# Eight layers on one core: the last sequence's state-space preparation under raised priority, and a softplus sum in another order

## The chip, the cores and the metric

The kernel runs on one core of a Trainium2 chip. Its engines are TensorE (PE, with its weight loads, PEld), VectorE (DVE), ScalarE (ACT), GpSimd (POOL) and SyncE (SP, which issues most DMAs). Each engine takes its instructions in the order in which the program lists them and waits on semaphores for the others. The metric is the device time of one execution in microseconds; the lower the better.

## The reference

A residual network of eight parts runs over x of 8 sequences x 256 positions x 128 channels, each followed by a layernorm of x + part(x): a gated linear recurrence, two layers of local attention, a selective state space, a mixture of 32 experts (top 1), attention in chunks, a mixture of 8 experts (top 2) with a shared expert, attention of typed heads and a ternary linear layer. The change touches the state space:

```python
xz = x @ W_in
x_inner, z = jnp.split(xz, 2, axis=-1)
xc = silu(causal depthwise convolution of x_inner, 4 taps, + conv_b)
x_ssm = xc @ W_xproj
delta_raw, Bm, Cm = x_ssm[..., :1], x_ssm[..., 1:17], x_ssm[..., 17:]
delta = jax.nn.softplus(delta_raw * w_dt + b_dt)
A = -jnp.exp(A_log)
dA = jnp.exp(delta[..., None] * A)
dBx = delta[..., None] * Bm[:, :, None, :] * xc[..., None]
# h = dA_t * h + dBx_t ;  y_t = sum_n h * C_t   over the 256 positions, 16 states
y = y + xc * D_param
y = y * jax.nn.silu(z)
return y @ W_out
```

## The kernel before

Channels lie on the 128 partitions and positions along the free dimension. One program runs six stages in a row; the change is in the second, `local_mamba`, in which the eight sequences pass through local attention and then the state space. Both are written as generators that yield their estimated cost; `interleave` runs four sequences of the first kind, staggered by 24, with up to two of the second behind them, and so sets the order in which instructions are written. A scheduler then gives every engine its own list: among the instructions that its model of the machine holds to be ready, it takes the one of the highest priority, which by default is the order of writing. `tc.high_priority()` raises the priority of what is issued inside it.

`mamba_sequence` (from L717) handles one sequence b. For both halves of 256 inner channels:

- L726 to L735: two matmuls into `xin`, then the convolution: ACT writes `xc` (L731), three DVE operations add the other taps (L733), first for one half, then for the other.
- L737 to L742: two matmuls into `z`, SiLU of `z` (`sz`) and of `xc` on ACT, then the loading of the exponential's table.
- L744 to L750: the 33 rows of x_ssm (`xps`, copied to `xs`), written to DRAM by SP.
- L761 to L778: `raw`, one matmul that spreads row 0 over all partitions, and the softplus. It is |v| and relu(v) for both halves (L767, L768: `e`, `r`), e = exp(-|v|) (L769), d = ln(1 + e) (L770), and a correction of the rounding in 1 + e: t = (e + 1) - 1 on DVE (L771), e = e - t, d = d + e, d = d + r, and u = d * xc. These last four (L774 to L778) run on POOL, but for the last sequence (b = 7) on DVE.
- L782 to L797, eight steps of two states each: SP fetches the rows of B and C from DRAM to all partitions (`bc`, 2 x 256 KB, three buffers, L758), ACT makes four `da` (L789, three buffers), DVE makes `hs` (L791), scans it (L793) and multiplies it by C (L794), PE adds it to `y`.
- L798 to L814: xc * D and SiLU of z (L800, L801), `wout`, the sum `s` (L806), a layernorm into `x_mamba`, and the router's logits (`lg`, L820).

Beside the last sequence runs `beside`: the folding of attention weights (`fold`, copied to `la_kq`, `la_vp`, `sa_kq`, `sa_vp` by ACT; `less`, `la_res`, `sa_res`), and, once sequence 6 is done, `route1` for its 14 tiles: comparisons on DVE (L961 to L967), a cumulative sum on PE (`cum`), transposes of the tiles (`rows`, L982, copied to `x_chunked` by ACT), the places (`put`, L993), and 14 indirect DMAs by POOL (L1088). After the last sequence `route1` runs once more for its two tiles; then SP and ACT load the experts' rows (`got`, L1108), and the stage `moe1` begins. SP also loads the expert weights (`w_moe`, L1135) in the order of writing.

Of the kernel before, what the change touches and what calls it, by code (L numbers as in the profile page):

```python
# [12 lines left out]
F32 = mybir.dt.float32  # L13
BF = mybir.dt.bfloat16
I32 = mybir.dt.int32
AF = mybir.ActivationFunctionType
ALU = mybir.AluOpType
# [4 lines left out]
P = 128  # L22
B = 8
S = 256
# [272 lines left out]
class _Kernel:  # L297
# [419 lines left out]
    def mamba_sequence(self, b, x, y, na, das, work, scan):  # L717


        nc = self.nc  # L720
        win = self.w1[:, 0:512]
        wx = self.w1[:, 512:578].rearrange("p (c f) -> p c f", c=2)
        wout = self.w1[:, 578:834].rearrange("p (c f) -> p c f", c=2)
        flat = lambda a: a.rearrange("p c s -> p (c s)")
        tile = lambda name, bufs=1: work.tile([P, 2, S], F32, tag="ma_" + name, name=name, bufs=bufs)
        ps = self.psum("M", "xin").rearrange("p (c s) -> p c s", c=2)  # L726
        for c in range(2):
            self.mm(ps[:, c, :], win[:, c * P : (c + 1) * P], x)
        xc = tile("xc", 2)
        for c in range(2):  # L730
            nc.scalar.activation(xc[:, c, :], ps[:, c, :], AF.Identity, scale=self.v("convw", 4 * c + 3), bias=self.v("convb", c))  # L731
            for k in range(1, 4):
                nc.vector.scalar_tensor_tensor(  # L733
                    xc[:, c, k:S], ps[:, c, 0 : S - k], self.v("convw", 4 * c + 3 - k), xc[:, c, k:S], ALU.mult, ALU.add
                )  # L735
        yield 2.0
        ps = self.psum("M", "z")  # L737
        for c in range(2):
            self.mm(ps[:, c * S : (c + 1) * S], win[:, 256 + c * P : 256 + (c + 1) * P], x)
        sz = tile("sz", 2)  # L740
        nc.scalar.activation(flat(sz), ps, AF.Silu)
        self.exp_ln(nc.scalar.activation(xc, xc, AF.Silu))  # L742
        yield 2.0
        ps = self.psum("M", "xps")  # L744
        for c in range(2):
            self.mm(ps[0:33, 0:S], wx[:, c, :], xc[:, c, :], c == 0, c == 1)
        xs = work.tile([33, S], F32, tag="xs", name="xs", bufs=2)
        nc.scalar.copy(xs, ps[0:33, 0:S])
        xd = self.dram.tile([33, S], F32, name=f"xs{b}")
        nc.sync.dma_start(xd, xs)  # L750

        def rows(m):

            bc = scan.tile([P, 2, 2, S], F32, tag="bc", name="bc", bufs=3)
            for k in range(2):
                r = 1 + 16 * k + 2 * m
                src = xd[r : r + 2, :].rearrange("n s -> (n s)").unsqueeze(0).to_broadcast([P, 2 * S])
                nc.sync.dma_start(bc[:, k].rearrange("p n s -> p (n s)"), src)  # L758
            return bc

        raw = self.psum("M", "raw")[:, 0:S]  # L761
        self.mm(raw, self.ident[0:33, 0:1].to_broadcast([33, P]), xs)
        yield 1.0

        e, r, d, t = tile("e"), tile("r"), tile("d", 2), tile("t")
        for c in range(2):
            nc.scalar.activation(e[:, c, :], raw, AF.Abs, scale=self.v("wdt", c), bias=self.v("bdt", c))  # L767
            nc.scalar.activation(r[:, c, :], raw, AF.Relu, scale=self.v("wdt", c), bias=self.v("bdt", c))  # L768
        nc.scalar.activation(e, e, AF.Exp, scale=-1.0)  # L769
        nc.scalar.activation(d, e, AF.Ln, bias=1.0)  # L770
        nc.vector.tensor_scalar(t, e, 1.0, -1.0, ALU.add, ALU.add)  # L771

        eng = nc.vector if b == B - 1 else nc.gpsimd
        eng.tensor_sub(e, e, t)  # L774
        eng.tensor_add(d, d, e)
        eng.tensor_add(d, d, r)
        u = tile("u", 2)
        eng.tensor_mul(u, d, xc)  # L778
        yield 3.0
        yp = self.psum("Y", "y")  # L780
        shp = [P, 2, 2, S]
        for m in range(8):  # L782
            bc = rows(m)
            bn, cn = (bc[:, k].unsqueeze(2).to_broadcast(shp) for k in range(2))
            da = das[m % len(das)]
            for n in range(2):
                for c in range(2):
                    i = 16 * c + 2 * m + n
                    nc.scalar.activation(da[:, n, c, 1:S], d[:, c, 1:S], AF.Exp, scale=na[:, i : i + 1])  # L789
            hs = scan.tile(shp, F32, tag="hs", name="hs", bufs=3)  # L790
            nc.vector.tensor_tensor(hs, u.unsqueeze(1).to_broadcast(shp), bn, ALU.mult)  # L791
            line = lambda a: a.rearrange("p n c s -> p (n c s)")
            nc.vector.tensor_tensor_scan(line(hs), line(da), line(hs), 0.0, ALU.mult, ALU.add)  # L793
            nc.vector.tensor_tensor(hs, hs, cn, ALU.mult)  # L794
            for n in range(2):
                self.mm(yp, self.ident, flat(hs[:, n]), m == 0 and n == 0, m == 7 and n == 1)
            yield 2.3  # L797
        yg = tile("t")  # L798
        for c in range(2):
            nc.vector.scalar_tensor_tensor(yg[:, c, :], xc[:, c, :], self.v("dpar", c), yp[:, c * S : (c + 1) * S], ALU.mult, ALU.add)  # L800
        eng.tensor_mul(yg, yg, sz)  # L801
        ps = self.psum("M", "wout")[:, 0:S]
        for c in range(2):
            self.mm(ps, wout[:, c, :], yg[:, c, :], c == 0, c == 1)
        s = work.tile([P, S], F32, tag="h2", name="s")
        nc.vector.tensor_add(s, ps, x)  # L806
        yield 2.0
        self.layernorm(work, s, y[:, bass.ts(b, S)])
        yield 2.0
        self.logits(b, y, self.w1[:, 834:866], self.lg1[0][:, 2 * b : 2 * b + 2] if b < 7 else self.lg1[1])  # L810
        self.done = b
        yield 1.0
# [1004 lines left out]
```

## Time and profile before

| | |
|---|---|
| Median of three runs | 1902.89 us (1902.8 to 1905.53) |
| Profiled execution | 1898.62 us, its span 1896.8 us |
| Mean granted clock of TensorE | 0.91 |
| Busy share of the span | PE 84%, PEld 50%, DVE 58%, ACT 54%, POOL 30% |
| Last scan step of sequence 6 multiplied by C (L794) | 839.2 us |
| First and last scan step of sequence 7 (L793) | from 861.95 us, to 898.3 us |
| First expert transposes | 921.33 us |

Times inside the profile are microseconds from the start of its span. A line of the order of time gives start, duration, engine, line, operation, output <- inputs, shapes, a count, and in brackets the idle time of the engine before it with what ended it. Matmuls of 32-bit data run in two passes, so a program's two matmuls appear as x4.

### The profile page before, as it was taken

The page shows a single profiled execution, that of the slowest core. Times are in us where ns is not written, and L with a number is a line of the kernel's source. Part 1 is how long each engine was busy: PE and PEld are TensorE (multiplying, and loading weights), DVE is VectorE, ACT ScalarE, POOL GpSimd, SP SyncE. Part 2 cuts the span into 40 slices and gives each one's busy share as a digit, 9 for nine tenths or more (in the row PEclk, how much of TensorE's full clock was granted, in tenths as well). Part 3 has the DMA queues.
Part 4 walks back from the last instruction along what each step waited for, and adds up shares of the span by engine and source line. Part 5 has one row for each costly group of instructions (what it writes and reads, how often), then busy time and mean ns, then how long its engine had stood idle before and what let it go on. Part 6 is the DMA issues. An engine that isn't in the chain of part 4 may idle for free. (4 is left out here: it accounts for less than half of the span.)

```text
span 1896.8 us, 28424 instructions
## 1 busy us (share of the span) xinstructions
PE 1585.0 (84%) x10810; PEld 957.3 (50%) x10810; DVE 1093.2 (58%) x2011; ACT 1020.7 (54%) x2702; POOL 560.4 (30%) x493
## 2 busy tenths in 40 slices
PE   3678887878788778786679999999988987899997
PEld 2344554535454444343656566665554733455554
DVE  5734458687779686679234554456443222467664
ACT  4557777667767877554234455444433312365654
POOL 1324443344342423203120211111111042255452
PEclk7789998989899988888789999999998997899998
DMA  4000002111112122366300000000101310000000
GB/s 172 1 1 1 1 35 56 35 56 35 45 46 56 35 56 68 95 215 167 102 24 2 10 6 6 6 5 5 36 2 29 104 39 13 1 4 4 7 4 9
DMA packets 58328, 75.50 MB, mean 40 GB/s; under 512 B 5868, under 2 KB 35236, under 8 KB 57168
## 3 DMA queue, kind: packets, MB, share of 16 engines
q1 hardware_dynamic: 52864, 67.57, 12.2%
q0 software_dynamic: 3216, 5.07, 0.9%
q8 instruction: 85, 1.39, 0.3%
q10 hardware_dynamic: 2112, 1.05, 0.2%
q14 instruction: 51, 0.42, 0.1%
HBM read 65.46 MB, written 9.71 MB: 40 GB/s over the span
## 5 line engine op out<-in xcount | busy, mean ns | idle before, releaser
L394 PE MATMUL y<-hs,ident 128*128 128x512 f32 x256 | 152.7, 727 | 38.0 <-DVE hs L794 37.8
L793 DVE TENSOR_TENSOR_SCAN hs<-da,hs 128x1024 f32<-128x1024 f32 x64 | 153.5, 2404 | 1.8 <-ACT da L789 1.6
L475 PE MATMUL pt<-ident,e 128*128 128x128 f32 x768 | 125.6, 291 | 23.7 <-POOL e L652 12.4
L652 POOL TENSOR_TENSOR e<-e,rc 128x1024 f32<-128x1024 f32 x32 | 67.9, 2121 | 232.6 <-DVE rc L651 232.6
L1686 ACT ACTIVATE e<-sc,nm 128x128 f32<-128x128 f32 (+1 forms) x256 | 104.1, 424 | 59.8 <-DVE nm L1681 57.5
L789 ACT ACTIVATE da<-d,na 128x255 f32<-128x255 f32 x256 | 111.8, 503 | 37.6 <-DVE hs L793 18.8
L1689 POOL TENSOR_TENSOR e<-e,rc 128x1024 f32<-128x1024 f32 x48 | 91.9, 1915 | 135.7 <-DVE rc L1688 102.4
L647 ACT ACTIVATE e<-sc,nm,rn 128x128 f32<-128x128 f32 x256 | 113.4, 462 | 24.9 <-DVE nm L642 22.4
L475 PEld LDWEIGHTS pt<-ident,e 128*128 128x128 f32 x768 | 90.2, 147 | 64.1 <-issue 22.4
L1298 POOL TENSOR_TENSOR e<-e,rc 128x512 f32<-128x512 f32 x32 | 33.5, 1048 | 295.7 <-DVE rc L1297 178.9
L599 POOL TENSOR_TENSOR t<-t,t 128x512 f32<-128x512 f32 x64 | 90.9, 1421 | 95.4 <-DVE t L586 79.0
L477 ACT COPY ptsb<-pt 128x512 f32<-128x512 f32 x94 | 55.1, 587 | 96.3 <-PE pt L475 87.5
L791 DVE TENSOR_TENSOR hs<-u,bc 128x1024 f32<-128x1024 f32 x64 | 86.2, 1357 | 34.0 <-POOL u L778 29.4
L394 PEld LDWEIGHTS y<-hs,ident 128*128 128x128 f32 x256 | 53.8, 226 | 97.6 <-DVE hs L794 51.7
L1273 ACT COPY kp<-kps 128x512 f32<-128x512 f32 x128 | 74.8, 584 | 41.7 <-PE kps L394 39.8
L1122 POOL DMA_INDIRECT got<-ybuf,get x48 | 45.5, 949 | 162.2 <-DMA ybuf<-ys 116.7
L477 DVE COPY ptsb<-pt 128x512 f32<-128x512 f32 x98 | 65.6, 685 | 33.5 <-PE pt L475 33.3
L394 PE MATMUL qk<-w_local,h 128*128 128x512 f32 x128 | 71.5, 648 | 14.1 <-DVE t L586 9.7
L794 DVE TENSOR_TENSOR hs<-hs,bc 128x1024 f32<-128x1024 f32 x64 | 80.0, 1256 | 0.2
L1246 DVE BATCH_NORM_STATS2 st<-out 128x6 f32<-128x128 f32 x80 | 20.0, 288 | 93.8 <-PE out L394 86.8
L1681 DVE TENSOR_REDUCE nm<-sc 128x4 f32<-128x1024 f32 (+1 forms) x48 | 58.6, 1220 | 24.6 <-PE sc L394 24.3
L1309 ACT COPY vs<-vps 128x512 f32<-128x512 f32 x64 | 37.4, 584 | 65.6 <-PE vps L394 44.1
(394 smaller groups left out, 3899.9 us busy)
## 6 DMA issues: line engine op xcount, KB each, us to landing
bc<-xs SPq DMA_DIRECT2D x128, 256.0 KB
w_attn<-in_w_dram SPq DMA_DIRECT2D x4, 1024.0 KB
w_local<-in_w_dram SPq DMA_DIRECT2D x2, 1557.0 KB
places<-zeros SPq DMA_DIRECT2D x2, 1280.0 KB
w_moe<-in_e1gate_dram SPq DMA_DIRECT2D x8, 256.0 KB
w_moe<-in_e1up_dram SPq DMA_DIRECT2D x8, 256.0 KB
w_moe<-in_e1down_dram SPq DMA_DIRECT2D x8, 256.0 KB
w_moe<-in_e2rg_dram SPq DMA_DIRECT2D x8, 256.0 KB
```

What stands on the lines that cost most here:

```text
L394: return self.nc.tensor.matmul(out, lhsT, rhs, start=start, stop=stop)
L475: self.last = self.nc.tensor.transpose(pt[:, j * P : (j + 1) * P], src[:, j * P : (j + 1) * P], self.ident)
L477: self.nc.any.tensor_copy(sb.rearrange("p a b -> p (a b)"), pt)
L599: nc.gpsimd.tensor_add(t1, t1, t2)
L647: nc.scalar.activation(e[:, j, g, :], scs[:, j, g, :], AF.Exp, bias=nm[:, j, g : g + 1], scale=rq[:, j, g : g + 1], accum_out=sm[:, j, g : ...
L789: nc.scalar.activation(da[:, n, c, 1:S], d[:, c, 1:S], AF.Exp, scale=na[:, i : i + 1])
L791: nc.vector.tensor_tensor(hs, u.unsqueeze(1).to_broadcast(shp), bn, ALU.mult)
L793: nc.vector.tensor_tensor_scan(line(hs), line(da), line(hs), 0.0, ALU.mult, ALU.add)
L794: nc.vector.tensor_tensor(hs, hs, cn, ALU.mult)
L1273: nc.scalar.copy(k[:, 2 * i : 2 * i + 2, :].rearrange("p a b -> p (a b)"), ps)
L1686: nc.scalar.activation(e[:, i, :], sc[:, i, :], AF.Exp, bias=nm[:, i : i + 1], accum_out=sm[:, i : i + 1])
L1689: nc.gpsimd.tensor_tensor(e, e, rc.unsqueeze(2).to_broadcast([P, n, keys]), ALU.mult)
```

## The change

For the last sequence (b = 7) the code up to `u` is put in `tc.high_priority()`; for the others the block is `ExitStack`, which does nothing. For all sequences the correction e - t is added to r, and that sum to d, where before it was added to d, and then r.

```diff
+        ahead = self.tc.high_priority if b == B - 1 else ExitStack
+        with ahead():
+            ps = self.psum("M", "xin").rearrange("p (c s) -> p c s", c=2)
...
         yield 2.0
-        ps = self.psum("M", "z")
...
+        with ahead():
+            ps = self.psum("M", "z")
...
+            self.exp_ln(nc.scalar.activation(xc, xc, AF.Silu))
         yield 2.0
...
+        with ahead():
+            ps = self.psum("M", "xps")
...
+            xd = self.dram.tile([33, S], F32, name=f"xs{b}")
+            nc.sync.dma_start(xd, xs)
...
+        with ahead():
+            raw = self.psum("M", "raw")[:, 0:S]
+            self.mm(raw, self.ident[0:33, 0:1].to_broadcast([33, P]), xs)
         yield 1.0
...
+        with ahead():
+
+            e, r, d, t = tile("e"), tile("r"), tile("d", 2), tile("t")
...
+            nc.scalar.activation(d, e, AF.Ln, bias=1.0)
+            nc.vector.tensor_scalar(t, e, 1.0, -1.0, ALU.add, ALU.add)
+
+            eng = nc.vector if b == B - 1 else nc.gpsimd
+            eng.tensor_sub(e, e, t)
-        eng.tensor_add(d, d, e)
-        eng.tensor_add(d, d, r)
+            eng.tensor_add(r, r, e)
+            eng.tensor_add(d, d, r)
+            u = tile("u", 2)
+            eng.tensor_mul(u, d, xc)
```

The lines between are the same, moved in by one level. The eight steps and what follows stand outside the block.

## The prediction

> **What bounds the kernel now.** I read the page first, then the busy time by stretch around the last sequence, then the order of work on DVE, PE and POOL there.
>
> ```profile
> span 1896.8 us, 28424 instructions
> ```
>
> The page's chain of waits reaches back from the end only to 1447 us, so for the place of the change I go by stretches (columns: stretch, length, then busy us of PE, PEld, DVE, ACT, POOL, then clock, DMA share, GB/s).
>
> ```profile
> 834.00:859.70 25.70, 19.43 (x118) 11.87 (x117) 15.72 (x28) 15.92 (x30) 1.26 (x1) 0.93 0.85 257
> 859.70:899.60 39.90, 27.87 (x92) 13.35 (x91) 39.82 (x41) 16.04 (x38) 15.31 (x9) 0.79 0.64 159
> ```
>
> The first row is the preparation of sequence 7, the second its eight scan steps. DVE is busy 39.82 of 39.90 us in the steps: they are bound by DVE, and no priority makes them shorter. In the preparation DVE has 25.70 - 15.72 = 10.0 us of idle time, and that is all that an earlier issue can win. DVE in order of time shows where it lies (start, us, instruction, idle time before it and who ended it):
>
> ```profile
> 844.10 0.48 DVE L800 SCALAR_TENSOR_TENSOR t<-xc,vec,y 128x256 f32<-128x256 f32 x1 [2.18 <-PE y L394]
> ...
> 847.99 0.42 DVE L806 TENSOR_TENSOR s<-wout,x_local 128x256 f32<-128x256 f32 x1 [2.24 <-PE wout L394]
> 853.20 0.42 DVE L441 TENSOR_TENSOR x_mamba<-ln,ln_rs 128x256 f32<-128x256 f32 x1 [4.78 <-ACT ln_rs L440]
> 853.79 0.43 DVE L771 TENSOR_SCALAR t<-e 128x512 f32<-128x512 f32 x1 [0.17 <-ACT e L769]
> ...
> 859.68 2.35 DVE L791 TENSOR_TENSOR hs<-u,bc 128x1024 f32<-128x1024 f32 x2
> ```
>
> Three waits (2.18, 2.24, 4.78) belong to the end of sequence 6 (y, wout, its layernorm), not to sequence 7. From 854.6 on DVE alternates the softplus of sequence 7 with the routing of the first 14 tiles, without a gap. PE beside it:
>
> ```profile
> 837.81 0.71 PE L394 MATMUL fold<-w_attn 64*128 64x128 f32 x6
> 840.47 3.60 PE L394 MATMUL y<-hs,ident 128*128 128x512 f32 x4 [1.95 <-DVE hs L794]
> ...
> 878.75 1.98 PE L394 MATMUL y<-hs,ident 128*128 128x512 f32 x4 [0.17 <-DVE hs L794]
> ...
> 894.81 3.68 PE L394 MATMUL y<-hs,ident 128*128 128x512 f32 x4 [2.59 <-DVE hs L794]
> 899.61 1.99 PE L394 MATMUL y<-hs,ident 128*128 128x512 f32 x4 [1.12 <-DVE hs L794]
> ```
>
> The same four y matmuls take 1.98 us or 3.6 us, by the granted clock (0.55 from 840.4 to 844.1, 1.00 before and after). And POOL:
>
> ```profile
> 795.64 1.27 POOL L774 TENSOR_TENSOR e<-e,t 128x512 f32<-128x512 f32 x1 [10.33 <-ACT d L770]
> ...
> 881.86 2.25 POOL L1088 DMA_INDIRECT places<-x_chunked,put  x1 [35.09 <-DVE put L993]
> ...
> 905.80 0.97 POOL L1088 DMA_INDIRECT places<-x_chunked,put  x1 [0.30 <-issue]
> 913.88 1.43 POOL L1088 DMA_INDIRECT places<-x_chunked,put  x1 [7.10 <-ACT lg L1006]
> ```
>
> The 14 early scatters end at 906.8; the last two tiles' scatters start 7.1 us later, so the early ones have slack. From the last scan step (899.6) to the first expert transposes (921.3) everything is one chain.
>
> **The softplus edit.** Four instructions before, four after, each 1.27 us on POOL (sequences 0 to 6) or 0.68 on DVE (7). Adding the correction to r instead of d would free the second instruction from the logarithm. But the first, e - t, writes e in place and must let the logarithm finish reading it: the POOL row waits for ACT's d. So nothing starts earlier: 0 us. The cover is that wait itself; if it were not there, one 1.27 us instruction for each of seven sequences could leave POOL's chain, 8.9 us at most, where DVE waits for u (4.48 us idle before the first hs of sequence 6, at 801.2). No extra cost is possible either: count, sizes and buffers are the same.
>
> **The priority edit.** The instruction orders of the two kernels differ only from the last scan steps of sequence 6 to the steps of sequence 7. On ACT, e, r, e, r and the exponential of sequence 7 no longer stand among the square and the two ln_rs of sequence 6. On DVE the four softplus operations and u come ahead of the copy of lg, and the routing of 14 tiles moves behind the first hs, one operation per step. On PE the tile transposes move up, between the folds and the last y. On SP one expert load moves ahead of the last four bc loads. I follow the chain with the durations of before:
>
> 1. The last y. la_res (0.27, DVE) moves ahead of the convolution, so hs ends at 840.6 and y can start at 840.65. In between PE now has four transposes (0.66) and one fold matmul, so its gap shrinks from 1.95 to about 1.0 us. Gaps of 0.17 and 1.12 were followed by 1.98 and 1.99, gaps of 1.95, 2.59 and 3.26 (at 826.8) by 3.60, 3.68 and 3.60; against this stands one start after 1.13 (867.6: eight in 5.41, half of it slow). I take the full clock: y ends at 842.6 instead of 844.1. The other bound is 844.25.
> 2. DVE takes t, xc, t, 0.39 apart as before: xc is whole at 843.6 (before 845.75), t at 843.9.
> 3. POOL's t (1.26) ends at 845.3, half of wout (0.5) at 845.85, xps (1.05) at 846.9. ACT has meanwhile done silu 0.63, a table load 1.28 and two la_vp copies (1.05), by 846.6. xs ends at 847.3 instead of 849.33: -2.0.
> 4. raw (0.69) ends at 848.05; the copy of the rows (0.58) fits beside it. e, r, e, r go 0.45 apart, then the exponential (0.63) ends at 850.6 instead of 853.69: -3.1. Here lies the gain of the priority: three ACT operations of some 0.3 us each are out of the way.
> 5. What comes later: ln_sq follows only then, the logarithm ends at 851.5. DVE: e - t from 851.55, three dependent operations of 0.70 to 853.65, x_mamba (0.35; its ln_rs is ready at 853.1), u (0.68) to 854.75. The copy of lg waits for two PE matmuls (0.63 after x_mamba): 854.95. The first hs starts then instead of at 859.68: -4.7.
> 6. Given back: the five routing operations that ran before the first hs (854.61 to 859.68, 0.54 each) now run in the steps: +2.7. Steps: 39.9 + 2.7 = 42.6, end 897.55 instead of 899.56.
>
> Sum: -4.7 + 2.7 = **-2.0 us**. With a slow last y all of it shifts by 1.6: -0.4.
>
> The queues. SP's first bc issue moves from 850.84 to 848.8, two 0.4 MB loads still ahead. DMA was busy until 859.3 for these 2.4 MB; in order, by the GB/s of each microsecond, the first two hs find their rows at about 852.5 and 854.6 and need them at 854.95 and 856.1. The expert load that now stands before bc of step 6 waits for the last `less`, behind the routing's cum matmuls: about 875, while that bc waits for hs of step 3 (876.6) anyway: 0. The put of the 14 tiles moves behind one more step (4.5 us): 883.4 instead of 880.8. POOL's scatters (24.9 us before) then end at 909.3, and the last two tiles' put comes at 913.0 - 2.0 = 911.0: hidden, slack 1.7 us.
>
> A rule that speaks against step 1: the Trainium skill, "TensorE: Matmul & The Clock Gate", section "What's actually happening", says that the clock falls to half only after an idle window of some 3.4 us. The row at 840.47 was slow after 1.95 us of idleness. By the rule the shorter gap would change nothing and the sum would be -0.4; by the rows it is -2.0.
>
> **Against the time.** The profiled execution took 1898.62, 1.8 outside its span; the median shown is 1902.89, so the profile lies 4.3 below it. -2.0 on the profile is 1896.6, on the median **1900.9**. About 0.2% (3.8 us) is what a measurement of this kernel tells from no change, so the forecast itself is "the same".
>
> **Rivals.**
> - *The wait moves to bc.* If the six bc loads share the queue instead of landing in order, all end near 859.3 - 2.0 = 857.3, and the first hs waits 2.35 us: -2.0 + 2.35 = +0.3, 1903.2. For it: DMA's share is near 1 from 851 to 858. Against it: bc of step 3, issued at 867.6, was there at 872.5 without a wait. A slow last y (-0.4, 1902.5) belongs here too: nothing comes through. 0.15.
> - *The clock gives more.* PE's expert groups from 923 to 930 take 1.9 us for eight matmuls, later ones 1.02. If the earlier, denser stretch leaves the clock up, two windows of 3.5 us at full rate instead of half give 2 x 1.75 more: -5.5, 1897.4. Against it: the order after the steps is unchanged, and PE is idle 9.4 us before the experts. 0.24.
> - *Slower: the scatters become the bound.* POOL's first six took 12.7 us (2.1 each, beside the expert loads), the rest 1.27 each. They now start at 884.4. From 1.96 us each on, the last two tiles' scatters wait for them (884.4 + 14 x 1.96 = 911.9); at 2.5 each they start at 919.4 instead of 913.9: +5.5, 1908.4. For it: the longest took 4.3 from start to start. Against it: the expert loads should end by about 892. 0.11.
>
> **How the numbers follow.** The forecast holds 0.50 (1899.5 to 1902.5, the rest of its spread being the clock's). Faster by over 0.2%: the second rival, and 0.04 of the forecast: 0.28. Slower: the third, 0.11. Within: 0.61. The range leaves about one in ten on each side: 1895.5 takes in the second rival, 1905.5 the first and the weak form of the third.
>
> **What would show it.** Right: the last y of sequence 6 at 2 us, the exponential ending about 3 us earlier and the first hs of sequence 7 nearly 5 us earlier than 859.68, but its last hs only 2 us earlier than 898.33; DVE without gaps between; the 14 scatters ending before the last put. Wrong: a DVE wait on a DMA at the first hs, PE's y still at 3.6 us, POOL starting the last two scatters without idle time, or a difference before 834 us, where the orders are equal but for the softplus's operands.

## The result, and the profile after

The changed kernel takes 1897.78 us (median of 20 runs, 1892.98 to 1908.92), the kernel before, beside it on the same chip, 1901.03 us (20 runs, 1897.78 to 1905.53). The ratio is 0.9986, 95% interval 0.9974 to 0.9997: some 3 us less, inside the 0.2% that a measurement of this kernel tells from no change. The profiled execution took 1892.98 us, the shortest of the twenty, 5.64 less than that of before.

```profile
span 1891.1 us, 28431 instructions
```

The busy time by stretch, cut at five events: the start of sequence 7's `x_local`, its first `hs`, the end of its last hs times C, the first expert transpose, and the end of the last expert product (columns: stretch, length, busy us of PE, PEld, DVE, ACT, POOL, then clock, DMA share, GB/s). First the changed kernel, then the kernel before at its own times of the same events.

```profile
833.20:855.20 22.00, 17.73 (x100) 10.66 (x100) 13.58 (x24) 15.27 (x29) 1.26 (x1) 0.96 0.95 286
855.20:897.73 42.53, 27.34 (x112) 14.35 (x112) 42.49 (x46) 16.46 (x39) 11.11 (x8) 0.82 0.60 161
897.73:921.53 23.80, 9.09 (x21) 4.32 (x22) 7.97 (x30) 3.10 (x6) 11.53 (x12) 0.57 0.14 38
921.53:948.22 26.69, 25.79 (x212) 24.81 (x212) 5.47 (x11) 10.82 (x20) 0.00 (x0) 0.93 0.58 157
```

```profile
833.65:859.68 26.03, 19.78 (x118) 11.87 (x117) 16.05 (x29) 15.90 (x30) 1.26 (x1) 0.93 0.86 259
859.68:899.56 39.88, 27.87 (x92) 13.35 (x91) 39.84 (x41) 16.05 (x38) 15.27 (x9) 0.79 0.64 159
899.56:921.33 21.77, 7.17 (x21) 3.61 (x22) 7.97 (x30) 3.10 (x6) 10.27 (x11) 0.63 0.14 40
921.33:951.65 30.32, 29.42 (x212) 28.44 (x212) 5.47 (x11) 10.82 (x20) 0.00 (x0) 0.82 0.52 139
```

Preparation 4.03 us shorter; steps 2.65 longer, with DVE full in both and five more instructions in them (46 for 41); the stretch to the first transposes 2.03 longer, at a clock of 0.57 for 0.63; the experts 3.63 shorter, at 0.93 for 0.82. So of the 5.7 us between the two spans, 1.38 are in the preparation and the steps, -2.03 in the tail and 3.63 in the experts. The rest, 0.45 ahead of the first stretch and 2.2 behind the last, lies where the change moves nothing.

DVE of the changed kernel in order of time (start, us, instruction, in brackets the idle time before it and who ended it):

```profile
842.23 0.48 DVE L807 SCALAR_TENSOR_TENSOR t<-xc,vec,y 128x256 f32<-128x256 f32 x1
...
847.30 0.42 DVE L813 TENSOR_TENSOR s<-wout,x_local 128x256 f32<-128x256 f32 x1 [3.81 <-PE wout L394]
850.71 0.43 DVE L778 TENSOR_SCALAR t<-e 128x512 f32<-128x512 f32 x1 [2.98 <-ACT e L776]
851.43 0.69 DVE L781 TENSOR_TENSOR e<-e,t 128x512 f32<-128x512 f32 x1 [0.29 <-ACT d L777]
...
853.49 0.42 DVE L441 TENSOR_TENSOR x_mamba<-ln,ln_rs 128x256 f32<-128x256 f32 x1
853.82 0.68 DVE L785 TENSOR_TENSOR u<-d,xc 128x512 f32<-128x512 f32 x1
855.06 0.23 DVE L827 COPY lg<-lg 128x64 f32<-128x64 f32 x1 [0.55 <-PE lg L394]
855.20 2.35 DVE L798 TENSOR_TENSOR hs<-u,bc 128x1024 f32<-128x1024 f32 x2
```

The 2.18 us wait for y is gone, the one for wout has grown from 2.24 to 3.81, the wait ahead of x_mamba has moved to the exponential (2.98) and the logarithm (0.29), and the first two hs run without a wait for bc. PE of the changed kernel around the two last steps:

```profile
840.21 1.98 PE L394 MATMUL y<-hs,ident 128*128 128x512 f32 x4 [0.53 <-DVE hs L801]
...
892.98 1.98 PE L394 MATMUL y<-hs,ident 128*128 128x512 f32 x4 [1.64 <-DVE hs L801]
897.78 3.68 PE L394 MATMUL y<-hs,ident 128*128 128x512 f32 x4 [2.81 <-DVE hs L801]
903.15 1.13 PE L394 MATMUL wout<-t,w 128*128 128x256 f32 x4 [1.69 <-DVE t L808]
...
921.53 1.94 PE L1122 MATMUL bt<-ident,got 128*128 128x128 f32 x8 [9.48 <-DMA got<-places]
```

The last y of sequence 6 fell from 3.60 to 1.98 us. The last y of sequence 7 rose from 1.99 to 3.68. Before, the y of the step ahead of it was the slow one and covered by DVE's scan; now the slow one is the y on which everything after hangs. The output projection starts at 903.15 us, for 903.28 before: of the 1.83 us by which the last hs*C ends earlier, 0.13 is left. POOL:

```profile
884.49 2.45 POOL L1095 DMA_INDIRECT places<-x_chunked,put  x1 [39.59 <-DVE sa_res L1227]
...
905.52 0.97 POOL L1095 DMA_INDIRECT places<-x_chunked,put  x1 [0.30 <-issue]
913.98 1.43 POOL L1095 DMA_INDIRECT places<-x_chunked,put  x1 [7.48 <-ACT lg L1013]
```

The 14 scatters end at 906.5 and leave 7.48 us of slack: they bind nothing.

### The profile page after: what moved, and what is told of

Its sections match the earlier page's. It is cut to its first block, busy times and chain, and to the rows that moved or that the text cites. A ratio compares the mean times of both kernels' runs of the same rounds, so it can differ in the third digit from the quotient of the medians.

```text
span 1891.1 us, 28431 instructions
## 1 busy us (share of the span) xinstructions
PE 1576.6 (83%) x10810; PEld 951.9 (50%) x10810; DVE 1094.1 (58%) x2011; ACT 1021.8 (54%) x2702; POOL 558.3 (30%) x493
## 4 chain that ended last, share of the span: by engine, by line
PE 53%; DVE 18%; ACT 11%; issue 8%; POOL 6%; another core or an unknown queue 2%; DMA 2%; POOLq 0%; DVEq 0%; SPq 0%; ACTq 0%
PE vps L394 7%; PE sc L394 7%; PE kps L394 6%; PE pt L475 4%; PE out L394 4%; PE o L394 4%; DVE hs L800 3%; PE pu L394 3%; PE pg L394 3%; ACT e L647 3%; DVE hs L801 2%; DVE hs L798 2%; PE hps L394 2%; PE py L394 2%
## 5 line engine op out<-in xcount | busy, mean ns | idle before, releaser
L394 PE MATMUL y<-hs,ident 128*128 128x512 f32 x256 | 148.5, 709 | 40.4 <-DVE hs L801 40.1
L475 PEld LDWEIGHTS pt<-ident,e 128*128 128x128 f32 x768 | 90.5, 147 | 64.1 <-issue 21.7
```

Source lines behind the costliest of these rows:

```text
L394: return self.nc.tensor.matmul(out, lhsT, rhs, start=start, stop=stop)
L475: self.last = self.nc.tensor.transpose(pt[:, j * P : (j + 1) * P], src[:, j * P : (j + 1) * P], self.ident)
```

## The experiments

They ran in three groups on three chips, on which the kernel before takes 1847 us (medians 1847.31, 1846.65 and 1847.85; e1 to e4, e5 to e7, e8 to e11). The difference from 1901 us lies behind the experts: 890.6 us from the last expert product to the end in the repeated profile of before, 945.1 in the first. The stretches studied here have the same lengths in both profiles of the kernel before (65.89 and 65.91, 21.87 and 21.77, 30.27 and 30.32 us), so all profiles can be set side by side. Each row's stretches come from one execution, its ratio from the medians of its group. "A" is the time from the start of sequence 7's `x_local` to the end of the last hs*C, "B" from there to the first expert transpose, "experts" from there to the end of the last expert product. The y columns give the last y of sequences 6 and 7 with the PE idle time before it.

| Kernel | y of 6 [gap] | A | y of 7 [gap] | B | experts | ratio, 95% interval |
|---|---|---|---|---|---|---|
| before | 3.60 [1.95] | 65.91 | 1.99 [1.12] | 21.77 | 30.32 | 1 |
| before, again (e11) | 3.58 [1.96] | 65.89 | 1.99 [1.11] | 21.87 | 30.27 | one run |
| changed | 1.98 [0.53] | 64.53 | 3.68 [2.81] | 23.80 | 26.69 | 0.9986 [0.9974, 0.9997] |
| changed, again (e8) | 1.98 [0.47] | 64.53 | 3.68 [2.81] | 23.74 | 26.77 | 1.0018 [1.0002, 1.0033] |
| e1, sum alone | 3.67 [1.88] | 65.99 | 1.99 [1.16] | 21.74 | 30.36 | 1.0008 [0.9994, 1.0021] |
| e2, priority alone | 1.98 [0.43] | 64.53 | 3.56 [2.81] | 23.49 | 30.22 | 0.9998 [0.9983, 1.0013] |
| e3, priority late | 1.98 [1.66] | 64.60 | 1.98 [1.03] | 21.95 | 30.28 | 0.9996 [0.9982, 1.001] |
| e4, priority early | 1.98 [0.50] | 64.40 | 3.59 [2.81] | 23.59 | 30.15 | 1.001 [0.9998, 1.0023] |
| e5, changed, filled at experts | 3.63 [0.43] | 66.42 | 1.98 [1.06] | 21.80 | 25.37 | 0.9977 [0.9962, 0.9992] |
| e6, before, filled at y of 6 | 1.98 [0.79] | 64.63 | 3.64 [2.81] | 23.66 | 30.10 | 0.9974 [0.9961, 0.9987] |
| e7, changed, filled at y of 7 and experts | 1.98 [0.43] | 64.54 | 1.98 [1.52] | 20.64 | 26.61 | 0.9966 [0.9951, 0.9981] |
| e9, before, filled at all three | 1.98 [0.79] | 64.63 | 1.99 [1.52] | 20.80 | 29.84 | 0.9975 [0.9955, 0.9994] |
| e10, e7 with five more | 1.99 [0.55] | 64.37 | 1.97 | 20.77 | 25.38 | 0.9969 [0.9951, 0.9987] |

**The parts of the change (e1 to e4).** First the sum alone, on the kernel before:

```diff
-        eng.tensor_add(d, d, e)
+        eng.tensor_add(r, r, e)
         eng.tensor_add(d, d, r)
```

> Before, with the correction added to r instead of d for all sequences, and no raised priority. The engines' orders are those of before. My theory (the edit is worth nothing, since e - t waits for the logarithm anyway): ratio 1.000 within its interval; the stretch from sequence 7's x_local (start of its layernorm product on DVE) to the end of its last hs * C stays at 65.9 us, as before (64.5 in the changed kernel); POOL's e - t still ends its wait on ACT's d. Rival (the freed order shortens POOL's chain in seven sequences): up to 8.9 us less, ratio down to 0.995, with the time before 834 us shorter.

A is 65.99 for 65.91, the ratio holds 1. The edit of the sum is worth nothing.

The priority alone, the changed kernel with the old sum:

```diff
-            eng.tensor_add(r, r, e)
+            eng.tensor_add(d, d, e)
             eng.tensor_add(d, d, r)
```

> The changed kernel with the old softplus sum: raised priority alone. My theory: the whole gain is here, ratio about 0.9985 (-2 to -3 us), the stretch from x_local to the last hs * C of sequence 7 at 64.5 us, first hs about 22 us after x_local (before: 26.0). Rival (both parts are needed, or the gain was the softplus's): ratio 1.000, stretch nearer to 65.9.

The same A as the whole change, the same slow y at the end of sequence 7, a ratio of 0.9998. What the change does, the priority does. But the experts took 30.22 us here, as in the kernel before, and not 26.69, and the whole kernel did not gain the 0.15% that was expected.

The priority for the later blocks alone (`raw` and the softplus), then for the earlier alone (`xin`, `z`, `xps`), both with the new sum. The two edits, against the changed kernel:

```diff
-        with ahead():
+        with ExitStack():
             ps = self.psum("M", "xin").rearrange("p (c s) -> p c s", c=2)
...
-        with ahead():
+        with ExitStack():
             ps = self.psum("M", "xps")
```

> The changed kernel with raised priority for raw and the softplus only (the last two blocks), not for the convolution, z and x_ssm. If the gain is ACT's order (e, r, e, r and the exponential ahead of sequence 6's layernorm, step 4 of the prediction) and the new order of DVE: the exponential ends some 1.1 us sooner after raw than before, and the stretch from x_local to the last hs * C is 65.9 - 0.4 to - 1.0 = about 65.2; the last y of sequence 6 is as slow as before where the gap ahead of it is 2 us. Rival (the gain is the earlier convolution and y): 65.9, nothing.

```diff
-        with ahead():
+        with ExitStack():
             raw = self.psum("M", "raw")[:, 0:S]
...
-        with ahead():
+        with ExitStack():
 
             e, r, d, t = tile("e"), tile("r"), tile("d", 2), tile("t")
```

> The changed kernel with raised priority for the convolution, z and x_ssm only (the first three blocks). If the gain is the last y of sequence 6 at full clock (step 1): y takes 2.0 instead of 3.6 us, everything up to the exponential comes about 1.6 us earlier, and the stretch is 65.9 - 1.4 = 64.5. If that y depends on the free phase of the clock and not on the order, the stretch is between 65.9 and 64.3, without relation to this edit. Rival (only the softplus block matters): 65.9 and the exponential where it was.

The first hs comes 21.89 us after x_local with the later blocks and 24.50 with the earlier ones, for 26.03 before. A is nevertheless 64.60 and 64.40: 2.6 us between the two starts of the steps and 0.2 between their ends. The y of sequence 6 was at full clock in both; for the later blocks a slow one and 65.2 had been expected. What brings the first hs forward does not decide when the last one ends; the question that is left is what does.

**The clock by itself (e5, e6).** In the next kernels constant matmuls stand in PE's idle time; their output is read by nobody.

```diff
+    def warm(self, tag, n, after=None):
+
+        ps = self.psum(tag, "warm")
+        for _ in range(n):
+            i = self.mm(ps, self.onesb, self.msk[:, 0:512])
+            if after is not None:
+                self.issue_after([i], after)
```

e6 is the kernel before with six of them behind the last scan of sequence 6, ahead of its y:

```diff
+            if b == B - 2 and m == 7:
+                self.warm("Q", 6, scanned)
```

> Before, with six matmuls of constants on PE ahead of the last y of sequence 6 (into a bank nobody uses then), nothing else changed. If the idle gap of 1.95 us is what sent that y to half clock (step 1): y takes 2.0 us, wout and xps of that moment come 1.5 us earlier, and the stretch from x_local to the last hs * C of sequence 7 falls from 65.9 to about 64.4; ratio about 0.999. Rival (the phase of the clock's window decides, or only an idle window of 3.4 us does): y at 3.6, stretch at 65.9.

PE and then DVE of e6:

```profile
838.25 1.46 PE L394 MATMUL warm<-msk,onesb 128*128 128x512 bf16 x6
841.35 1.98 PE L394 MATMUL y<-hs,ident 128*128 128x512 f32 x4 [0.79 <-DVE hs L802]
...
899.22 3.64 PE L394 MATMUL y<-hs,ident 128*128 128x512 f32 x4 [2.81 <-DVE hs L802]
```

```profile
854.22 0.62 DVE L971 TENSOR_REDUCE route<-lg 128x14 f32<-128x448 f32 x1
854.76 0.68 DVE L782 TENSOR_TENSOR e<-e,t 128x512 f32<-128x512 f32 x1
855.36 0.62 DVE L972 TENSOR_TENSOR oh<-lg,route 128x448 f32<-128x448 f32 x1
...
858.16 0.68 DVE L786 TENSOR_TENSOR u<-d,xc 128x512 f32<-128x512 f32 x1
858.76 0.62 DVE L977 TENSOR_TENSOR sel<-route_tables,route 128x448 bf16<-128x448 f32 x1
859.30 2.35 DVE L799 TENSOR_TENSOR hs<-u,bc 128x1024 f32<-128x1024 f32 x2
```

DVE still alternates softplus and routing, as the kernel before does, and the first hs comes at 24.76 us. Yet A is 64.63, the changed kernel's 64.53 within 0.1: the clock of this one y gives the whole gain in A, without any priority. The order of e6 is that of e1, whose y was slow, and the clock's changes lie at the same place in both (last section), so it is the six matmuls that made the difference. It also brings the changed kernel's slow y at the end of sequence 7 and its B (23.66).

e5 is the changed kernel with 28 such matmuls ahead of the expert transposes:

```diff
             groups = 0
+            self.warm("M", 28)
```

> The changed kernel with 28 matmuls of constants (128x512, bf16, into a free bank, read by nobody) on PE between the last cumulative sum and the first expert transposes, where PE was idle for 9.4 us. If the clock at the experts' start depends on PE's idleness before it: the experts' first ten groups of eight matmuls run at 1.05 us from the start instead of 1.9 (before: 10 us of them, changed kernel's profile: 3.5 us), the experts' stretch (first transposes to the last py) is about 25 us instead of 30.3 and 26.7, and the ratio to before is 0.9986 less 1.7 to 5 us, about 0.997. Rival (the half clock there has another cause, or the matmuls come too late and push the transposes back): no change against the changed kernel, ratio 0.9986 or above.

The experts fell to 25.37 us, at a clock of 1.00. Besides, this execution shows the missing corner of the comparison, in PE's order of time:

```profile
844.67 3.63 PE L394 MATMUL y<-hs,ident 128*128 128x512 f32 x4 [0.43 <-DVE hs L809]
...
904.13 1.98 PE L394 MATMUL y<-hs,ident 128*128 128x512 f32 x4 [1.06 <-DVE hs L809]
```

Here the changed kernel's order met a slow y at sequence 6. A is 66.42, of which 0.58 is a wait of the second hs for bc; 65.84 without it (a difference, not a measurement), no better than before. So there are four corners, the last from this one execution: with y fast 64.63 (order before) and 64.53 (order after), with y slow 65.9 and 66.42, or 65.84 without the wait. The order is worth 0.1 us, the clock of y 1.3.

**The tail held up as well (e7, e9, e10).** e7 is the changed kernel with six ahead of the last y of sequence 7 and 28 ahead of the experts:

```diff
+            if b == B - 1 and m == 7:
+                self.warm("Q", 6, scanned)
...
             groups = 0
+            self.warm("M", 28)
```

> The changed kernel with the 28 matmuls ahead of the experts and six more ahead of the last y of sequence 7. If the last y's 3.68 us in the changed kernel's profile was the idle gap of 2.8 us before it: y takes 2.0, the stretch from the last hs * C to the first expert transposes falls from 23.8 to about 21.8, and the ratio is 1 to 2 us below the one with the 28 alone. Rival (the six come in the way, y starting later than hs * C allows): the same stretch or longer.

```profile
897.70 1.46 PE L394 MATMUL warm<-msk,onesb 128*128 128x512 bf16 x6
900.67 1.98 PE L394 MATMUL y<-hs,ident 128*128 128x512 f32 x4 [1.52 <-DVE hs L809]
...
911.63 7.64 PE L394 MATMUL warm<-msk,onesb 128*128 128x512 bf16 x28
921.26 1.81 PE L1132 MATMUL bt<-ident,got 128*128 128x128 f32 x8 [1.98 <-DMA got<-places]
```

y is back at 1.98 us and B falls to 20.64, 3.1 us below the changed kernel's and 1.2 below what was expected. The ratio 0.9966 is the lowest of the study (1840.12 us).

e9 is the kernel before, in its own order, with six matmuls ahead of the last y of sequence 6 and of sequence 7 and 28 ahead of the experts:

```diff
+            if b >= B - 2 and m == 7:
+                self.warm("Q", 6, scanned)
...
             groups = 0
+            self.warm("M", 28)
```

> The kernel before, in its own order of issue, with six constant 128x512 bf16 matmuls ahead of the last y of sequences 6 and 7 and 28 ahead of the expert transposes; their output is read by nobody. Theory (with PE's clock held up in both orders, the raised priority is worth nothing, since what it moves ahead of the first hs is DVE work that comes back inside the steps): the last hs*C ends 64.6 us after x_local, as in the earlier run with the matmuls at sequence 6 alone (64.63), the first bt 20.6 to 21.3 us later, and the ratio equals that of the changed kernel with such matmuls (0.9966) within its interval, 0.9975 to 0.9955. Rival (the priority is worth its 2 us whatever the clock): the last hs*C 66 us after x_local although y takes 1.98 us, and the time 2 us above that of the changed kernel with such matmuls.

A is 64.63 and B 20.80, together 85.43 for e7's 85.18. With the clock held up at both y in one profile of each, priority and sum together are worth 0.25 us. The ratio, 0.9975, holds e7's within its interval. The experts stayed slow in its profile (29.84): the transposes came 2.19 us after the last constant matmul and ran at half clock, 1.94 us, so these 28 are no sure cure.

e10 is e7 with five more behind the last y, ahead of the output projection:

```diff
+            if b == B - 1 and m == 7:
+                self.warm("Q", 5, added)
```

> The changed kernel with six constant matmuls ahead of the last y of sequence 7, five more behind it, ahead of the output projection, and 28 ahead of the expert transposes; their output is read by nobody. Theory (from the last scan step on each gap of PE costs by the clock of the next small matmuls): the output projection shortens from 1.1 to 0.7 us, the stretch from the last hs*C to the first bt falls from 20.64 to about 20.0 us, ratio 0.9963, between 0.9978 and 0.9948. Rival (the stretch is bound by ACT and DVE, and the matmuls only stand in front of the projection): 20.6 us or more, ratio 0.9966 or above.

```profile
910.11 1.24 PE L394 MATMUL warm<-msk,onesb 128*128 128x512 bf16 x5
911.97 1.13 PE L394 MATMUL wout<-t,w 128*128 128x256 f32 x4 [0.61 <-DVE t L820]
```

The projection stayed at 1.13 us in spite of a gap of 0.61, B at 20.77, the ratio at 0.9969. The five bring nothing, as the rival had it. There was nothing for them to bring: the granted clock at the projection was already 1.00 in e7, where it took the same 1.13 us. What binds this stretch was not taken apart.

**The two kernels again (e8, e11).** No edit.

> The changed kernel itself, beside the other kernels of this call. Theory (all that comes through of the preparation is the clock of the last y of sequence 6; the tail gives it back by the clock of the last y of sequence 7): ratio to before 0.999, between 0.998 and 1.000; from the start of sequence 7's x_local the last hs*C ends after 64.5 us if the last y of sequence 6 takes 1.98 us, after 66 us if it takes 3.6. Rival (the 2.0 us of the prediction come from the order on ACT and DVE, not from the clock): 64.5 us or less in either case.

> The kernel before once more, for a second profile of it. Theory (in its order PE is idle for 1.9 us ahead of the last y of sequence 6, and this is enough for half clock there): y at 3.6 us, the last hs*C ends 65.9 us after x_local, the first bt 21.8 us later, the experts 30.3 us. Rival (the clock there is chance): y at 1.98 us and 64.6 us.

Both stretches repeat to 0.1 us. The time does not follow as expected: 1.0018 for the changed kernel, with an interval that does not meet the first one's. The order of instructions of the changed kernel has thus been timed three times (with e2), at 0.9986, 0.9998 and 1.0018. The two profiles of before show one source of such a spread: the same code reached `x_local` of sequence 7 after 833.65 us in one and 842.46 in the other, 8.8 us apart, ahead of everything that the change moves. What makes that difference was not looked into. The three together do not show the change to be faster or slower; its size lies below 0.2%.

The other ratios are to be read with the same care. From x_local to the end of the experts, e5 is 4.4 and e7 6.2 us shorter than the kernel before (118.00), and their medians are 3.25 and 6.53 lower; but e6 is 0.4 us longer there, and its median is 4.54 lower. That e7 is faster than the kernel before has e10 beside it, 0.9969 in another group, in which the changed kernel came out at 1.0018; how much of it is the matmuls is shown for the stretches, not for the whole kernel.

## Why the prediction was right, and where not

The forecast, no measurable change and -2.0 us from the median, stood on a first hs that comes much earlier and steps that give most of it back. That holds.

- **Step 1, the y.** Full clock by a shorter gap: y ended at 842.19 us, predicted 842.6; the gap was 0.53 us, predicted 1.0. It was also at full clock in e2, e3, e4, e7, e8 and e10, where the order has the whole of the priority or a part of it and nothing is filled in at this y. It was slow in e5, after a gap of only 0.43 us, and at the next-to-last step of sequence 7 it was fast after 3.58 us (e6, e9) and slow after 1.42 (e3, e10). As a rule on gaps step 1 is therefore too simple: what goes with a slow y, in all but a few rows, is how little PE did in the 3.41 us piece of the clock ahead of it: 1.60 us before, 2.72 in the changed kernel (last section). The shorter gap was a sign of that.
- **The rule weighed against step 1.** The Trainium skill, "TensorE: Matmul & The Clock Gate", section "What's actually happening", lets the clock fall after an idle window of some 3.4 us; read as a window without any work, this would have given -0.4. The runs decide for the rows: 1.3 us came from shortening a gap of under 2 us, in the changed kernel and in e6.
- **Steps 2 to 5.** From x_local on, xs began 13.47 us later, for 15.32 before (-1.85, predicted -2.0), the exponential ended after 17.40 for 20.04 (-2.64, predicted -3.1), and the first hs came after 22.00 for 26.03 (**-4.03, predicted -4.7**). e6, with only y fast, splits it: its first hs is at 24.76, so 1.27 us of the 4.03 are the clock of y, and 2.76 the order of issue.
- **Step 6, given back.** 2.65 us, predicted 2.7: the five routing operations now stand in the steps, the first of them at 864.10 us. Against the 2.76 us that the order brings, this is all of it but 0.1. The term that was mis-sized is the order's part of step 5: predicted some 3.2 us (4.7 less y's 1.5), measured 2.76.
- **The sum on the last hs*C**: predicted -2.0, measured -1.38 from x_local on.
- **The term that was missing** is behind the steps. I held that all from the last scan step to the experts is one chain and left its length as it was. It is one chain, but its first link is a y whose clock goes by how busy PE was just before: +1.69 us at the y, +2.03 in B. In the piece of the clock ahead of it PE was busy for 0.60 of 3.41 us in the changed kernel, for 3.40 of 3.40 before, where the slow y of the step ahead filled it, and for 1.89 in e7 with the six matmuls. It is not the order within the steps that did this: e6 has the order of before there, and the same slow y (3.64). The steps ended earlier, and so their y came to lie differently against the clock's pieces; in e3 and e5, where the pieces lie differently again, the changed order, or a part of it, has a fast y. In all profiles with no constant matmuls at the last y of sequence 7, B is 21.7 to 22.0 where that y was fast and 23.5 to 23.8 where it was slow. I used the rows with 1.12 and 2.59 us of idle time ahead of y to argue for step 1, and did not apply them to the other end of the steps.
- **The rival of the clock** (-5.5, through two windows of full clock more at the experts) came true in part in the profiled execution: 3.63 us less there. But with the same order e2 took 30.22 us and e8 26.77, and PE was idle for 9.4 us ahead of the transposes in each. So the earlier, denser stretch does not bring it; it differs between executions of the same order, and goes with where the transposes fall between the clock's changes (last section).
- **Rivals that fell.** bc: no wait at the first two hs in the changed kernel, one of 0.58 us in e5. The scatters: 22.0 us for 14, with 7.48 us to spare. The put was predicted for 883.4 and came at 883.43. The price of that rival was misread: the 12.7 us (881.86 to 894.58) are five scatters from start to start, 2.5 us each, not six of 2.1.
- **The softplus edit**: predicted 0, e1 shows 1.0008 [0.9994, 1.0021] and an A that differs by 0.08 us. That its cover is the logarithm's reading of e is argued from the code and the order; in e1 POOL's e - t still waits for the logarithm, as before (10.34 us, ended by ACT's d), but no run takes that wait away.
- **The sign "a difference before 834 us"** can't serve: two profiles of the kernel before differ there by 8.8 us.

So the time came out as forecast partly by luck, since errors made up for one another: the scan end gained 0.6 us less than predicted, the tail lost 2.0 us that were not predicted, and the experts' clock, in that execution, gave 3.6. The medians' difference, 3.25 us, can't be split in this way, since a profile is one execution.

## What to carry to other kernels

Where one engine is full through a stretch, work that is moved ahead of another on it comes back inside that stretch: count the operations moved, and expect the difference of the ends, not of the starts. Where a chain enters and leaves such a stretch through short bursts of matmuls, ask for each end separately which burst will be at half clock, because what brings one forward moves the other against the clock's changes; in e6 six matmuls at the entry alone slowed the exit. Before giving a reordering the credit, hold the clock equal in both orders with a few constant matmuls in the idle time; here, in one profile of each, that left 0.25 us of difference.

## What the runs showed of the hardware

The half clock comes in pieces of 3.41 us or multiples of it. In each of the thirteen profiles all changes of the granted clock lie on one grid of that step, which lies differently against the program from one execution to the next. In most cases the clock of a piece goes by how long PE was busy, in sum, in the piece ahead of it. The rows below are cut at this grid, in each pair the piece ahead of the last y of sequence 6 and the piece of that y: the kernel before, the changed kernel, e6 and e5.

```profile
836.92:840.33 3.41, 1.60 (x10) 0.83 (x8) 3.41 (x3) 1.48 (x3) 0.00 (x0) 1.00 1.21 293
840.33:843.74 3.41, 3.27 (x4) 1.41 (x5) 1.15 (x4) 1.05 (x2) 0.00 (x0) 0.50 1.11 400
```

```profile
836.37:839.78 3.41, 2.72 (x15) 1.41 (x13) 3.41 (x4) 2.92 (x5) 0.00 (x0) 1.00 1.17 288
839.78:843.19 3.41, 2.98 (x18) 1.64 (x18) 2.69 (x7) 0.56 (x1) 0.00 (x0) 1.00 1.10 385
```

```profile
837.97:841.38 3.41, 2.62 (x15) 1.20 (x12) 3.41 (x4) 0.79 (x2) 0.00 (x0) 1.00 1.14 282
841.38:844.79 3.41, 2.96 (x10) 1.36 (x10) 1.92 (x6) 1.57 (x4) 0.01 (x1) 1.00 1.04 348
```

```profile
841.45:844.86 3.41, 2.40 (x15) 1.42 (x14) 3.41 (x4) 2.41 (x5) 0.00 (x0) 1.00 1.08 276
844.86:848.27 3.41, 3.41 (x6) 0.88 (x5) 1.12 (x3) 0.56 (x1) 0.00 (x0) 0.50 1.02 367
```

In the first three the piece ahead begins at nearly the same place, 3.27, 3.17 and 3.43 us after the start of x_local; in e1, with the order of before and a slow y, it begins at 3.41 and PE is busy in it for 1.53 us. So there it is the work in the piece that differs, not the place of the grid. In e5 the piece begins at 3.80 us, and half clock followed although PE was busy for 2.40 us of it.

Over all thirteen profiles, a piece at full clock in which PE was busy for less than 40% was followed by half clock in 340 of 340 cases, from 40 to 50% in 125 of 181, from 50 to 80% in 40 of 879 (e5's is one of them), above 80% in none of 4528. From half clock the next piece was again at half in 412 of 412 cases below 75%, and in 157 of 652 above. So the busy time decides nearly all cases; what else counts in the remaining ones, these runs leave open.

An idle time that lies across a change of piece can therefore pass without harm. In e10 PE did nothing for 3.41 us on end (833.56 to 836.97), and the clock stayed at 1.00 for the y behind it (1.99 us): the idle time lay in two pieces, in which PE was busy for 1.68 and 1.67 us. The same y with a gap of 3.26 us ran at half clock in the changed kernel's second profile (3.61 us), where the piece ahead had PE busy for 0.26 us.

Pieces of 3.41 us agree with the window that the Trainium skill, "TensorE: Matmul & The Clock Gate", section "What's actually happening", names; it also calls it free-running, as the grids here are. If that section is read to mean a wholly idle window, the rows do not bear it out.

The place of the grid also goes with the experts' time where nothing was filled in or the fill ended too early: 26.6 to 26.8 us where the transposes began 0.15 to 0.35 us ahead of a change of piece (the changed kernel twice, and e7), 29.8 to 30.4 in the eight other profiles. No run set this place on purpose, so that it is the cause is not shown.
